# A gate/up pass of a fused transformer kernel from 12-bit parts, with the parts made one pass earlier by ScalarE and accumulating DMAs

## The chip, the cores and the metric

The kernel runs on one core of one Trainium2 chip. A core has five engines with queues of their own: TensorE (PE; its weight loads are shown as PEld), VectorE (DVE), ScalarE (ACT), GpSimd (POOL) and SyncE (SP, which here only issues DMAs). The metric is the time of one execution in microseconds on the device; lower is better. Before the change three runs took 990.1, 990.8 and 993.25 us, median 990.8.

## The reference

Four rows `x[b]` of 512 tokens by 256 channels pass through four residual blocks: a windowed attention with a small convolution (A), a feed-forward block (FFN), a 16-head causal attention (B), and the same FFN with the same weights again.

```python
def _L0_ffn_ref(x, gate_W_packed, gate_scales, up_W_packed, up_scales, down_W_packed, down_scales):
    Wg = dequant_nvfp4(gate_W_packed, gate_scales)
    Wu = dequant_nvfp4(up_W_packed, up_scales)
    Wd = dequant_nvfp4(down_W_packed, down_scales)
    gate = jnp.einsum('th,nh->tn', xt, Wg)
    up = jnp.einsum('th,nh->tn', xt, Wu)
    gelu = jnp.tanh(0.7978845608028654 * (gate + 0.044715 * gate ** 3)) * gate * 0.5 + gate * 0.5
    inter = gelu * up
    out = jnp.einsum('tn,hn->th', inter, Wd)

x = x + _L0_attn_a_ref(_layernorm(x, axis=-1), ...)
x = x + _L0_ffn_ref(_layernorm(x, axis=-1), ...)
x = x + _L0_attn_b_ref(_layernorm(x, axis=-1), ...)
x = x + _L0_ffn_ref(_layernorm(x, axis=-1), ...)
```

The weights are 256 x 2048 (gate, up) and 2048 x 256 (down), everything in float32.

## The kernel before

**Passes.** One FFN pass treats one row b. Its 2048 hidden values are 16 blocks n of 128. For each n there is a gate tile and an up tile of 128 x 512, each summed over two halves `par` of the 256 channels; then gelu on ScalarE (`gs`), a product on VectorE (`it`), and after every eight blocks the down product in four groups of 64/4 matmuls (`po`), added to `X[b]` by VectorE (L977). There are eight passes: f0 to f3 after attention A, and s0 to s3 after attention B.

**Two ways to multiply.** The function `ffn` (from L901) multiplies float32 weights from SBUF directly: the raw weights `Wf["g"]` and `Wf["u"]`, 16 tiles of 128 x 512, named by matrix, `par` and quarter q of the hidden values. f0, f1 and f2 run so. In the other way every factor is split into parts of about 12 bits, in a type that TensorE takes in one go: `high = w * NEAR` rounded, the rest `w - high`, and a correction `w - high * (1 + STEP)`. A tile is then four matmuls (`begin`: forms 0 and 1, two `par` each), a scaling of the PSUM bank by ScalarE (1 + STEP), and two matmuls with form 2 on top (`end`). The activations are split in the same manner into `xs`. f3 and all of s0 to s3 run so, inside `conduct` (`ffn_pass`, L1243 on), with weights read back from DRAM as chunks of 768 KB, one for each n.

**Where the parts come from.** `keep_parts` (L989) takes the 16 raw tiles; ScalarE writes `high` (L997), VectorE the two others (L998, L999), and SyncE stores each as 256 KB into the DRAM tensor `kept` (L1001). Its steps stand beside f2 and window 3. Their room is one slot of the tag "T".

**Order.** `weave` takes work of attention A ("window" b+1) and of the pass f_b together: every step of the window yields a time, and TensorE gets main work for as long. Beside f1 stands window 2, beside f2 window 3. Only TensorE's order is written out there (`manual_schedule(engines=PE_ONLY)`); the framework orders the other engines' queues when the program is built. The window's VectorE half is `window_middle`; its yields are 46.2 us in sum, scaled by (0.79, 1.24, 1.22) for windows 1, 2 and 3. Then come `project` (L714, L720), `turn` (L739, L741), `move` (TensorE, zp, L761), `add` (VectorE, L772) and `norm_rows`, in which GpSimd computes an inverse root (`inv_root`, L102 and L103) and TensorE transposes the normalized rows (L886) that ScalarE copies to `xT` (L892). The next window's `window_front` has a root of its own on GpSimd (L352).

**PSUM.** Until the end of f2 the pool `fbank` has three banks, afterwards four.

```python
        with tc.manual_schedule(engines={mybir.EngineType.PE, mybir.EngineType.DVE}):
            first_slot()
        for b in range(1, 3):
            weave(ffn(f1, i1, b, got[b], f"f{b}", False, False), beside_window(b + 1), 1.0)
```

Of the kernel before, what the change touches and what calls it, by code (L numbers as in the profile page):

```python
# [18 lines left out]
P = 128  # L19
# [20 lines left out]
def hybrid_kernel(  # L40
# [50 lines left out]
    def hold(pool, names):  # L91
        for name in names:
            Wf[name] = [[pool.tile([P, 512], F32, name=f"{name}{par}_{q}") for q in range(4)] for par in range(2)]

    hold(wpool, "d")
    store = ctx.enter_context(tc.tile_pool(name="store", bufs=1, space=bass.MemoryType.DRAM))
# [889 lines left out]
                    )  # L986


    def keep_parts(make):  # L989

        for q in range(4):
            for k, mat in enumerate(("g", "u")):
                for par in range(2):
                    w = Wf[mat][par][q]
                    t = make(f"{mat}{par}_{q}")
                    top = t[:, 0].bitcast(F32)
                    nc.scalar.activation(t[:, 0], w, AF.Copy, scale=NEAR)  # L997
                    nc.vector.tensor_tensor(t[:, 1], w, top, ALU.subtract)  # L998
                    nc.vector.scalar_tensor_tensor(t[:, 2], top, -1.0 - STEP, w, ALU.mult, ALU.add)  # L999
                    for form in range(3):  # L1000
                        nc.sync.dma_start(  # L1001
                            out=kept[q][:, :, k, form, par, :].rearrange("n p c -> p n c"),
                            in_=t[:, form].bitcast(F32).rearrange("p (n c) -> p n c", c=P),
                        )
                    yield 0.0

    class Slot:

# [762 lines left out]
    def scaled(work, by):  # L1771
        for w in work:
            yield w * by
# [31 lines left out]

    got, mine, state = [], [], {}
    with ExitStack() as left:
        hold(left.enter_context(tc.tile_pool(name="wraw", bufs=1, side="left")), "gu")
        aw = left.enter_context(tc.tile_pool(name="aw", bufs=1, side="left"))
        a1 = left.enter_context(tc.tile_pool(name="a1", bufs=1, side="left"))  # L1810
        a2 = left.enter_context(tc.tile_pool(name="a2", bufs=2, side="left"))
# [211 lines left out]
        def beside_window(b):  # L2023

            middle = window_middle(a1, a2, wconst, b, state)
            other = iter(())
            if b + 1 < B:
                xa = window_load(a2, b + 1)
                other = window_front(a1, a2, wconst, b + 1, xa, state)

            if b == 3:
                room = a2.tile([P, 2, 4, 512], F32R, tag="T", name="room")
                made = []

                def make(name):
                    made.append(name)
                    return room[:, len(made) % 2, 0:3]

                other = keep_parts(make)
            yield from between(  # L2040
                scaled(middle, (0.79, 1.24, 1.22)[b - 1]), until(other, state, b + 1) if b + 1 < B else other
            )
            project, turn, move, add = window_back(a1, a2, wconst, b, state)
            for hf in range(2):
                yield from project(hf)
            wait = sum(turn())
            if b + 1 < B:
                next(other)
                wait = 3.5
            yield wait  # L2050
            move()
# [12 lines left out]
        for b in range(1, 3):  # L2064
            weave(ffn(f1, i1, b, got[b], f"f{b}", False, False), beside_window(b + 1), 1.0)

    early.close()
    fbank = ctx.enter_context(tc.tile_pool(name="ps4", bufs=4, space=bass.MemoryType.PSUM))
# [96 lines left out]
```

## Time and profile before

| What | us |
|---|---|
| Median of three runs | 990.8 |
| The profiled execution, its own time | 993.88 |
| its span in the profile | 992.0 |
| f1's first gate matmul | 189.9 |
| f2's first gate matmul | 290.9 |
| f2's last down matmul ends about | 383.2 |
| Parts: first activation, last store issued | 262.3, 342.7 |
| First chunk load of f3 issued | 376.8 |

Mean granted TensorE clock of the execution: 0.991. Line numbers are those of the kernel before. A line of a timeline gives start, length, engine, line, operation, output and inputs, and in brackets the idle time of the engine just before and what ended it. Matmuls are pipelined, so the starts of successive groups tell the pace, not their lengths. Tile names end in the stage: `_f` for f0 to f3, `_s` for s0 to s3. A 128 x 512 float32 matmul counts as two instructions, so a full tile shows as x4; a tile from parts shows as x4 (`begin`) and x2 (`end`).

### The profile page before, as it was taken

How to read it: one execution, taken by the hardware profiler on the slowest of the kernel's cores; microseconds unless marked ns; L12 is line 12 of the kernel's file. 1: busy time of each engine (PE TensorE's matmuls, PEld its weight loads, DVE VectorE, ACT ScalarE, POOL GpSimd, SP SyncE). 2: the span in 40 equal slices, each digit the busy share in tenths (PEclk: the TensorE clock that was granted, in tenths of full speed). 3: DMA queues.
4: the chain of work that ended last, by engine and by line, in shares of the span. 5: the costliest groups of instructions: out<-in, count | busy, mean ns of one | idle time of the engine just before them, and what ended most of it. 6: DMA issues, size and time to landing. Idle time of an engine off the chain costs nothing.

```text
span 992.0 us, 15580 instructions
## 1 busy us (share of the span) xinstructions
PE 960.7 (97%) x5872; PEld 654.0 (66%) x5872; DVE 713.6 (72%) x1626; ACT 454.4 (46%) x806; POOL 137.0 (14%) x263
## 2 busy tenths in 40 slices
PE   8999998999999999899999999999999999999998
PEld 6874647655674666666556666676666677657887
DVE  7889998889899767875876776667775667546211
ACT  3453243040333111665462853746727548475531
POOL 2100000010000013201422123111141111120000
PEclk9899999999999999999999999999999999999999
DMA  5202110000245605331330340522503406134730
GB/s 147 93 25 62 41 45 1 23 1 0 67 124 146 175 12 185 128 128 50 103 104 1 107 149 1 191 76 75 191 1 128 139 11 212 44 128 143 251 124 34
DMA packets 51774, 90.92 MB, mean 92 GB/s; under 512 B 4915, under 2 KB 37963, under 8 KB 51667
## 3 DMA queue, kind: packets, MB, share of 16 engines
q1 hardware_dynamic: 49696, 89.34, 27.8%
q8 instruction: 46, 0.75, 0.3%
q10 hardware_dynamic: 1906, 0.54, 0.2%
q14 instruction: 30, 0.24, 0.1%
q0 software_dynamic: 96, 0.05, 0.1%
HBM read 75.24 MB, written 14.68 MB: 91 GB/s over the span
## 4 chain that ended last, share of the span: by engine, by line
PE 80%; DVE 11%; ACT 4%; DMA 2%; issue 1%; SPq 0%; POOL 0%; DVEq 0%; ACTq 0%
PE po_s L1325 11%; PE pg_f L913 7%; PE pu_f L934 6%; PE pg_s L1269 6%; PE pu_s L1269 6%; PE s L1540 5%; PE po_f L962 4%; PE sT L1574 4%; PE o L1618 4%; PE pu_s L1282 3%; PE qk_b L1453 3%; PE po_f L1325 3%; PE pg_s L1282 3%; PE va L496 2%; PE pg_f L1269 2%; PE v_b L1485 1%
## 5 line engine op out<-in xcount | busy, mean ns | idle before, releaser
L1554 DVE CUSTOM_DVE_ANT_0 junk<-s,mask 128x512 f32<-128x512 f32 (+3 forms) x256 | 125.6, 491 | 54.3 <-PE s L1540 20.7
L1325 PE MATMUL po_s<-d,it_s 128*128 128x256 f32 x512 | 117.8, 383 | 0.6 <-DVE it_s L1312 0.5
L1325 PEld LDWEIGHTS po_s<-d,it_s 128*128 128x128 f32 x512 | 95.3, 190 | 20.4 <-issue 5.2
L1586 ACT ACTIVATE e<-sT 128x1024 f32<-128x1024 f32 (+1 forms) x66 | 64.7, 1006 | 88.7 <-PE sT L1574 88.6
L1593 POOL TENSOR_SCALAR_AFFINE_SELECT e<-e 128x256 f32<-128x256 f32 x128 | 53.4, 429 | 336.9 <-ACT e L1586 311.2
L913 PE MATMUL pg_f<-xT_f,g 128*128 128x512 f32 x192 | 93.1, 607 | 1.0 <-ACT xT_f L889 0.7
L934 PE MATMUL pu_f<-xT_f,u 128*128 128x512 f32 x192 | 91.1, 593 | 0.0
L962 PE MATMUL po_f<-d,it_f 128*128 128x256 f32 x384 | 88.6, 387 | 0.5 <-DVE d L830 0.4
L962 PEld LDWEIGHTS po_f<-d,it_f 128*128 128x128 f32 x384 | 72.9, 193 | 13.3 <-issue 1.8
L925 ACT ACTIVATE gs_f<-pg_f 128x512 f32<-128x512 f32 x48 | 28.6, 595 | 109.9 <-PE pg_f L913 102.3
L1269 PE MATMUL pg_s<-xs_s,chunk_s 128*128 128x512 f32 x256 | 70.8, 398 | 0.5 <-ACT qT L1517 0.5
L1269 PE MATMUL pu_s<-xs_s,chunk_s 128*128 128x512 f32 x256 | 70.7, 398 | 0.5 <-DVE gu_s L1310 0.5
L913 PEld LDWEIGHTS pg_f<-xT_f,g 128*128 128x128 f32 x192 | 35.9, 193 | 44.9 <-issue 35.2
L934 PEld LDWEIGHTS pu_f<-xT_f,u 128*128 128x128 f32 x192 | 36.0, 191 | 42.3 <-issue 40.2
L1269 PEld LDWEIGHTS pu_s<-xs_s,chunk_s 128*128 128x128 f32 x256 | 47.1, 188 | 18.0 <-DVE it_s L1312 1.7
L1269 PEld LDWEIGHTS pg_s<-xs_s,chunk_s 128*128 128x128 f32 x256 | 46.9, 188 | 14.8 <-ACT qT L1517 1.3
L1274 ACT ACTIVATE pu_s<-pu_s 128x512 f32<-128x512 f32 x64 | 37.3, 583 | 41.2 <-PE pu_s L1269 40.4
L1540 PE MATMUL s<-kT,qT 16*128 16x256 f32 (+3 forms) x512 | 50.9, 467 | 3.2 <-ACT qT L1517 1.9
L1296 DVE SCALAR_TENSOR_TENSOR g_s<-g_s,gs_s 128x512 f32<-128x512 f32 x48 | 33.6, 701 | 20.5 <-ACT g_s L1294 20.5
L1274 ACT ACTIVATE pg_s<-pg_s 128x512 f32<-128x512 f32 x64 | 37.3, 583 | 21.5 <-PE pg_s L1269 20.9
L1618 PE MATMUL o<-e,V 128*32 128x256 f32 (+3 forms) x512 | 44.4, 442 | 0.0
L1282 PE MATMUL pu_s<-xs_s,chunk_s 128*128 128x512 f32 x128 | 41.9, 408 | 1.1 <-ACT pu_s L1274 1.1
(281 smaller groups left out, 1739.6 us busy)
## 6 DMA issues: line engine op xcount, KB each, us to landing
chunk_s<-kept SPq DMA_DIRECT2D x64, 768.0 KB
kept<-room SPq DMA_DIRECT2D x48, 256.0 KB
chunk_f<-kept SPq DMA_DIRECT2D x16, 768.0 KB
X<-in_x_dram SPq DMA_DIRECT2D x4, 512.0 KB
out_dram<-X SPq DMA_DIRECT2D x15, 128.0 KB
xa<-in_x_dram SPq DMA_DIRECT2D x28, 64.0 KB
pkg<-in_gate_p_dram SPq DMA_DIRECT2D x4, 256.0 KB
sbg<-in_gate_s_dram SPq DMA_DIRECT2D x4, 256.0 KB
```

What stands on the lines that cost most here:

```text
L913: nc.tensor.matmul(pg, Wf["g"][par][q][:, o : o + P], xT[:, par, :], start=par == 0, stop=par == 1)
L934: nc.tensor.matmul(pu, Wf["u"][par][q][:, o : o + P], xT[:, par, :], start=par == 0, stop=par == 1)
L962: nc.tensor.matmul(po[:, 0:W], inter[k][:, i * P : (i + 1) * P], Wf["d"][par][j // 2][:, (j % 2) * W : (j % 2 + 1) * W], start=k == 0, sto ...
L1269: nc.tensor.matmul(ps(), ch()[:, int(mat == "u"), form, par], xs()[:, form, par], start=k == 0, stop=k == 3)
L1274: step("ACT", 0.585, lambda: nc.scalar.activation(ps(), ps(), AF.Copy, scale=1.0 + STEP), r=[ps], w=[ps], lane="ffn", rank="scale")
L1282: nc.tensor.matmul(ps(), ch()[:, int(mat == "u"), 2, par], xs()[:, 2, par], start=False, stop=par == 1, skip_group_check=True,)
L1325: nc.tensor.matmul(po()[:, 0:W], inter[n]()[:, i * P : (i + 1) * P], Wf["d"][par][j // 2][:, (j % 2) * W : (j % 2 + 1) * W], start=k == 0, ...
L1540: nc.tensor.matmul(pss[hl // 2]()[:, hl % 2, p0 : p0 + n], qT[h0 : h0 + HD, g, i * P : (i + 1) * P], kT[h0 : h0 + HD, g, 0:n], start=True, ...
L1554: step("DVE", 0.155 + n / 960.0 + 0.085, lambda hl=hl, i=i, p0=p0, n=n, h=h, junk=junk: nc.vector.tensor_tensor_reduce(out=junk()[:, 0:n], ...
L1586: step("ACT", 0.16 + 2 * total / 1200.0, lambda: nc.scalar.activation(e()[:, :, 0:total], pss[k]()[:, :, at0:512], AF.Exp), r=[(pss[k], "t ...
L1593: nc.gpsimd.affine_select(out=diag, in_=diag, pattern=[[0, 2], [1, P]], compare_op=ALU.is_ge, fill=0.0, base=0, channel_multiplier=-1,)
L1618: nc.tensor.matmul(o()[h0 : h0 + 32, kt * P : 512], c["V"][:, kt, 4 * g + hl, :], e()[:, hl % 2, p0 : p0 + n], start=kt == 0, stop=kt == 2,)
```

## The change

f2 is run from parts too, by a new generator `ffn_in_parts`. The parts are made beside f1 and window 2 instead of beside f2 and window 3. `keep_parts` no longer uses VectorE: ScalarE makes `less = -high`, `high` and `low = -STEP * high`, SyncE stores them, and GpSimd's queue then adds the raw weight to form 1 in DRAM and form 1 to form 2 in DRAM, by two accumulating DMAs per raw tile. The 16 raw tiles lie in a pool whose tags are reused: the first six hold the room of `xs`, three groups of three that of the three chunk buffers of f2, and one stands alone. Window 3's middle is scaled by 1.05 instead of 1.22.

```diff
+    def hold_in_turn(pool):
+
+        turns = [(name, par, q) for q in range(4) for name in "gu" for par in range(2)]
+        first = pool.tile([P, 6, 512], F32, tag="xs", name="raw_first")
+        rest = [pool.tile([P, 3, 512], F32, tag="chunk", bufs=3, name=f"raw{k}") for k in range(3)]
+        last = pool.tile([P, 512], F32, name="raw_last")
+        spots = [first[:, k] for k in range(6)] + [t[:, k] for t in rest for k in range(3)] + [last]
...
-    def keep_parts(make):
+    def keep_parts(pool):
 
         for q in range(4):
             for k, mat in enumerate(("g", "u")):
                 for par in range(2):
                     w = Wf[mat][par][q]
-                    t = make(f"{mat}{par}_{q}")
-                    top = t[:, 0].bitcast(F32)
-                    nc.scalar.activation(t[:, 0], w, AF.Copy, scale=NEAR)
-                    nc.vector.tensor_tensor(t[:, 1], w, top, ALU.subtract)
-                    nc.vector.scalar_tensor_tensor(t[:, 2], top, -1.0 - STEP, w, ALU.mult, ALU.add)
-                    for form in range(3):
-                        nc.sync.dma_start(
-                            out=kept[q][:, :, k, form, par, :].rearrange("n p c -> p n c"),
-                            in_=t[:, form].bitcast(F32).rearrange("p (n c) -> p n c", c=P),
-                        )
+                    to = [kept[q][:, :, k, form, par, :].rearrange("n p c -> p n c") for form in range(3)]
+                    of = lambda t: t.rearrange("p (n c) -> p n c", c=P)
+                    high = pool.tile([P, 512], F32R, tag="g2", name=f"high_{mat}{par}_{q}")
+                    less = pool.tile([P, 512], F32R, tag="gu", name=f"less_{mat}{par}_{q}")
+                    low = pool.tile([P, 512], F32, tag="gu", name=f"low_{mat}{par}_{q}")
+                    nc.scalar.activation(less, w, AF.Copy, scale=-NEAR)
+                    nc.sync.dma_start(out=to[1], in_=of(less.bitcast(F32)))
+                    nc.scalar.activation(high, w, AF.Copy, scale=NEAR)
+                    nc.sync.dma_start(out=to[0], in_=of(high.bitcast(F32)))
+                    nc.scalar.activation(low, high.bitcast(F32), AF.Copy, scale=-STEP)
+                    nc.sync.dma_start(out=to[2], in_=of(low))
+                    nc.gpsimd.dma_start(out=to[1], in_=of(w), accum_op=ALU.add)
+                    nc.gpsimd.dma_start(out=to[2], in_=to[1], accum_op=ALU.add)
                     yield 0.0
+
+    def in_parts(pool, xT, name):
+
+        xs = pool.tile([P, 3, 2, 512], F32R, tag="xs", name=f"xs_{name}")
+        part = xs.bitcast(F32)
+        for par in range(2):
+            nc.scalar.activation(xs[:, 0, par], xT[:, par], AF.Copy, scale=NEAR)
+            nc.vector.tensor_tensor(xs[:, 2, par], xT[:, par], part[:, 0, par], ALU.subtract)
+            nc.scalar.activation(xs[:, 1, par], part[:, 2, par], AF.Copy, scale=4096.0)
+            nc.vector.tensor_tensor(xs[:, 2, par], part[:, 0, par], part[:, 1, par], ALU.subtract)
+        return xs
+
+    def ffn_in_parts(pool, ipool, ring, b, xT, name, tanh, last):
+
+        xs = in_parts(ring, xT, name)
+        chunks = {}
+
+        def begin(mat, n):
+            if n not in chunks:
+                chunks[n] = ring.tile([P, 2, 3, 2, P], F32R, tag="chunk", bufs=3, name=f"chunk_{name}_{n}")
+                nc.sync.dma_start(out=chunks[n].bitcast(F32), in_=kept[n // 4][n % 4])
+            ps = fbank.tile([P, 512], F32, tag="ps", name=f"p{mat}_{name}_{n}")
+            for k, (form, par) in enumerate(((0, 0), (0, 1), (1, 0), (1, 1))):
+                nc.tensor.matmul(
+                    ps, chunks[n][:, int(mat == "u"), form, par], xs[:, form, par], start=k == 0, stop=k == 3
+                )
+            nc.scalar.activation(ps, ps, AF.Copy, scale=1.0 + STEP)
+            return ps
+
+        def end(mat, n, ps):
+            for par in range(2):
+                nc.tensor.matmul(
+                    ps, chunks[n][:, int(mat == "u"), 2, par], xs[:, 2, par],
+                    start=False, stop=par == 1, skip_group_check=True,
+                )
...
+                    if begun:
+                        close()
+                        yield 0.45
+                    begun = mat, n, ps
...
-        hold(left.enter_context(tc.tile_pool(name="wraw", bufs=1, side="left")), "gu")
+        wraw = left.enter_context(tc.tile_pool(name="wraw", bufs=1, side="left"))
+        hold_in_turn(wraw)
...
-            yield from between(
-                scaled(middle, (0.79, 1.24, 1.22)[b - 1]), until(other, state, b + 1) if b + 1 < B else other
-            )
+            beside = between(scaled(middle, (0.79, 1.24, 1.05)[b - 1]), until(other, state, b + 1) if b + 1 < B else other)
+            yield from between(beside, keep_parts(f1) if b == 2 else iter(()))
...
-        for b in range(1, 3):
-            weave(ffn(f1, i1, b, got[b], f"f{b}", False, False), beside_window(b + 1), 1.0)
+        weave(ffn(f1, i1, 1, got[1], "f1", False, False), beside_window(2), 1.0)
+        weave(ffn_in_parts(f1, i1, wraw, 2, got[2], "f2", False, False), beside_window(3), 1.0)
```

The lines left out of `ffn_in_parts` are the gelu (ScalarE), the product `it` (VectorE) after each `end`, as in `ffn`, and the call of `down` after eight blocks. Each `begin` yields 0.91 us, each `end` 0.45.

More of the change, by code (lines that the diff above doesn't have):

```diff
@@ L93, in hold @@
             Wf[name] = [[pool.tile([P, 512], F32, name=f"{name}{par}_{q}") for q in range(4)] for par in range(2)]
+    def hold_in_turn(pool):
[4 more added lines that the diff above has]
+        spots = [first[:, k] for k in range(6)] + [t[:, k] for t in rest for k in range(3)] + [last]
+        for name in "gu":
+            Wf[name] = [[None] * 4 for _ in range(2)]
+        for (name, par, q), spot in zip(turns, spots):
+            Wf[name][par][q] = spot
     hold(wpool, "d")
@@ new lines, in ffn_in_parts, with close @@
+    def ffn_in_parts(pool, ipool, ring, b, xT, name, tanh, last):
[18 more added lines that the diff above has]
+                )
+        for half in range(2):
+            inter, gates, begun = [], {}, None
+            def close():
+                mat, n, ps = begun
+                end(mat, n, ps)
+                if mat == "g":
+                    gs = pool.tile([P, 512], F32, tag="gs", name=f"gs_{name}_{n}")
+                    g2 = None
+                    if tanh:
+                        nc.scalar.copy(gs, ps)
+                        g2 = pool.tile([P, 512], F32, tag="g2", name=f"g2_{name}_{n}")
+                        nc.scalar.activation(g2, gs, AF.Square, scale=0.044715 ** 0.5)
+                        nc.vector.scalar_tensor_tensor(g2, g2, 1.0, gs, ALU.add, ALU.mult)
+                        nc.scalar.activation(g2, g2, AF.Tanh, scale=0.7978845608028654)
+                    else:
+                        nc.scalar.activation(gs, ps, AF.Gelu_apprx_tanh)
+                    gates[n] = gs, g2
+                else:
+                    gs, g2 = gates.pop(n)
+                    it = ipool.tile([P, 512], F32, tag="it", name=f"it_{name}_{n}")
+                    if tanh:
+                        gu = pool.tile([P, 512], F32, tag="gu", name=f"gu_{name}_{n}")
+                        nc.vector.scalar_tensor_tensor(gu, ps, 0.5, gs, ALU.mult, ALU.mult)
+                        nc.vector.scalar_tensor_tensor(it, g2, 1.0, gu, ALU.add, ALU.mult)
+                    else:
+                        nc.vector.tensor_tensor(it, ps, gs, ALU.mult)
+                    inter.append(it)
+            for n in range(8 * half, 8 * half + 8):
+                for mat in ("g", "u"):
+                    ps = begin(mat, n)
+                    yield 0.91
+                    if begun:
+                        close()
+                        yield 0.45
+                    begun = mat, n, ps
+            close()
+            yield 0.45
+            for _ in down(b, name, half, inter, last):
+                yield 0.86
@@ L2029, in beside_window @@
                 other = window_front(a1, a2, wconst, b + 1, xa, state)
[L2031 to L2039, printed above, removed]
-            yield from between(
-                scaled(middle, (0.79, 1.24, 1.22)[b - 1]), until(other, state, b + 1) if b + 1 < B else other
-            )
+            beside = between(scaled(middle, (0.79, 1.24, 1.05)[b - 1]), until(other, state, b + 1) if b + 1 < B else other)
+            yield from between(beside, keep_parts(f1) if b == 2 else iter(()))
             project, turn, move, add = window_back(a1, a2, wconst, b, state)
```

## The prediction

> **What bounds the kernel now.** I read the page's first two parts, then the chain of waits, then stretches of the span by engine, then TensorE's, VectorE's and GpSimd's own timelines at the places that the change touches.
>
> ```profile
> PE 960.7 (97%) x5872; PEld 654.0 (66%) x5872; DVE 713.6 (72%) x1626; ACT 454.4 (46%) x806; POOL 137.0 (14%) x263
> ...
> PE 80%; DVE 11%; ACT 4%; DMA 2%; issue 1%; SPq 0%; POOL 0%; DVEq 0%; ACTq 0%
> ```
>
> TensorE is busy 97% of the span and holds 80% of the chain that ends last: time is won where TensorE's work shrinks, if nothing else then ends later. In the stretches of the second pass (189 to 290) and the third (291 to 382) the columns are length, then busy time of PE, PEld, DVE, ACT and POOL, granted clock, DMA share, GB/s:
>
> ```profile
> 189.00:262.00 73.00, 73.00 (x307) 41.97 (x307) 63.43 (x107) 22.09 (x39) 3.06 (x1) 1.00 0.00 1
> 262.00:290.00 28.00, 26.87 (x280) 21.05 (x279) 27.23 (x44) 8.55 (x14) 1.20 (x2) 0.94 0.50 142
> 290.00:330.00 40.00, 39.53 (x117) 21.30 (x116) 40.00 (x58) 14.18 (x20) 0.00 (x0) 1.00 0.46 132
> 330.00:370.00 40.00, 40.00 (x245) 23.05 (x244) 24.45 (x44) 8.88 (x15) 0.97 (x1) 1.00 0.30 86
> ```
>
> VectorE is full from 262 to 330, yet TensorE loses only 1.13 us up to 290 and 0.47 in the next 40. GpSimd is nearly empty. So the third pass is paced by matmuls, with VectorE as a close second.
>
> **Fewer passes through the array: -11.5 us.** TensorE's timeline (start, length, instructions), first in the second pass, then in a pass from parts in the tail:
>
> ```profile
> 232.15 1.88 PE L913 MATMUL pg_f<-xT_f,g 128*128 128x512 f32 x4
> 233.87 1.88 PE L934 MATMUL pu_f<-xT_f,u 128*128 128x512 f32 x4
> ```
> ```profile
> 957.29 1.07 PE L1269 MATMUL pg_s<-xs_s,chunk_s 128*128 128x512 f32 x4
> 958.20 0.62 PE L1282 MATMUL pu_s<-xs_s,chunk_s 128*128 128x512 f32 x2
> 958.65 0.61 PE L1269 MATMUL pu_s<-xs_s,chunk_s 128*128 128x512 f32 x2
> ```
>
> A full tile takes 233.87 - 232.15 = 1.72 us, a tile from parts 958.65 - 957.29 = 1.36. The pass has 32 gate and up tiles: 32 x 0.36 = 11.5 us less. The down half (13.81 us per 64 matmuls) is untouched.
>
> **VectorE's share of the parts goes: -2.9 us.** Today 32 VectorE instructions at about 0.69 us (22 us in all) make the parts, nine of them between 267 and 278. They stand in front of the residual addition:
>
> ```profile
> 270.43 0.69 DVE L998 TENSOR_TENSOR room<-u,room 128x512 fp32r<-128x512 f32 x1
> 271.04 1.21 DVE L772 TENSOR_TENSOR X<-X,zp 128x1024 f32<-128x1024 f32 x1
> ```
> ```profile
> 272.31 1.02 PE L426 MATMUL qkv<-bw,yT 32*128 32x96 f32 x26 [1.13 <-DVE X L772]
> ...
> 274.43 9.72 PE L962 MATMUL po_f<-d,it_f 128*128 128x256 f32 x36
> ```
>
> TensorE waits 1.13 us for that addition, and the clock then sags (0.71, 0.50 and 0.94 in the 2 us slices from 274 to 280): 36 down matmuls span 283.99 - 274.43 = 9.56 us, where 36/64 x 13.81 = 7.8 are due. The zp matmuls end at 268.87 and no part would stand in between, so 1.1 + 1.8 us should return; bounds 0 and 2.9, I take 2.9.
>
> **The new beginning of the pass: +1.5.** Four ScalarE and four VectorE instructions split xT ahead of the first matmul. The fourth pass has the same chain: its first split begins at 381.40 and its last needed one ends at 384.57, 3.2 us. Today xT of the third pass is copied by 287.81 and the first pg starts at 290.92: 3.1 us of cover from the second pass's last down matmuls. If VectorE is in a 2.28 us product (L535) at both subtractions, 4.6 us show. Bounds 0 and 5; nearest to the covered case, so 1.5.
>
> **Three banks, now coupled more tightly: +3.** Today a pu bank is asked for again two tiles later, 3.44 us after its last matmul. From parts, one begin (0.91) and one end (0.45) lie between: 1.36 us for VectorE to see it, multiply (0.69) and free it. Products of 1.2 to 2.3 us fill VectorE in the first half of the pass, so a multiply can miss by up to about 0.9 us. Eight tiles at 0.4 give 3. Bounds: 0 (VectorE is some 7 us further ahead than today, ten part instructions fewer by 293) and 7 (eight at 0.9). ScalarE's scaling (0.585) must fit under the next begin, 0.91. Four table loads of 1.28 us lie between 287.8 and 301.9, three of them in the pass, and each now sits in front of a scaling: 0 to 4, I take 1.5.
>
> **The ring has three chunks: +0.5.** A chunk is free one begin and one end after its own pair (4.08 us after its first matmul) and its buffer is due again at 8.16. In the tail the last chunk is issued at 964.28 and DMA activity is over at 968 (share 0.87, then 0.03): about 4.0 us against 4.08. Bounds 0 and 2.
>
> **The end of the pass: +2.** After window 3's last matmuls (zp, ended 368.88) 13.0 us of down work (60 matmuls) cover a fixed chain: addition, norm, and transfers of attention weights that land at 382.3. The middle's factor 1.22 to 1.05 on 46.2 us of yields holds window 3 back less (48.5 us instead of 56.4); with 13.2 us of later yields 61.7 of 71.1 us of pass are spent before zp, 9.4 us stay. 13 - 9.4 = 3.6 us of cover are missing. Bounds 0 and 4 (a new idle may bring its own sag); norm work placed there fills some, so 2.
>
> **The parts beside the second pass: +1, if GpSimd keeps up.** ScalarE gets 48 activations at 0.63 us, 30 us, in a phase where it is busy some 31 of 101: room enough, but each `less` waits until the store before has left its buffer (two stores, issued at 262.93 and 263.44, are through by 266: about 2.5 us), and the xT, aT and gelu copies queue behind it; 0 to 5. SyncE issues 48 stores as before, earlier, behind window 3's xa loads (179.7 to 185.5, needed at 191.4), and 16 chunk loads more behind them. The heavy item is GpSimd's queue: 32 accumulating transfers, the second of each pair waiting for the first to land, ahead of window 3's root (204.4, with 1.7 us until VectorE uses it) and of the third pass's own:
>
> ```profile
> 1.37 0.84 POOL L173 DMA_DIRECT2D wrep<-in_qkv_w_dram  x1 [0.37 <-issue]
> ...
> 2.56 0.61 POOL L175 DMA_DIRECT2D sh<-in_shift_dram  x1
> 3.16 0.63 POOL L198 DMA_DIRECT2D prep<-in_proj_w_dram  x1
> ```
> ```profile
> 276.33 0.20 POOL L102 TENSOR_SCALAR rs_f<-mv_f 128x4 f32<-128x4 f32 x1 [68.83 <-DVE mv_f L849]
> 276.61 1.01 POOL L103 TENSOR_TENSOR rs_f<-rs_f,mhalf 128x4 f32<-128x4 f32 x1
> ```
>
> No accumulating transfer is in this trace. Nearest are GpSimd's three plain ones of 128 rows: 0.61 to 0.84 us to issue, 2.6 to 4.5 us to land. Ours have 512 pieces of 512 B and 256 KB, 0.91 us at the 287 GB/s that the stores reached. Issue: 0.6 (one per transfer) to 2.5 (four times 0.63); taken 1.3. Landing: 2.6 to 6.3 (4.5 and the data twice); taken 4.2. A step of two: 3.2 to 8.8, taken 5.5; sixteen from 189.9 end at 241, 278 or 331. The root at 276.33 has 4.9 us of slack (factors applied by 279.03, transposes in TensorE's order at 283.99), so 281.2 is the deadline, 5.7 us per step: the value taken is in time by 3 us.
>
> On this the Trainium skill's page "SBUF — State Buffer", section "SBUF: two separate sides", speaks against the change: while VectorE runs an instruction that takes both ports, GpSimd can't write descriptors, and an issue of 620 ns became 3100. By it, 32 issues alone would be an estimated 99 us, past the deadline. This trace's nearest row is the root at 204.4, 3.06 us beside a full VectorE against 1.68 at 10.2, and no transfer of GpSimd lies beside dense VectorE work, so I keep the sum by rows.
>
> **Sum.** -11.5 - 2.9 + 1.5 + 3 + 1.5 + 0.5 + 2 + 1 = -4.9. The profiled execution took 993.88 us (span 992.0 and 1.9 around it), 3.1 over the median of 990.8; 993.88 - 4.9 = 989.0 there, 985.9 on the median: **986**. Differences under 0.3% (3 us, 987.8 to 993.8) can't be told from none.
>
> **Rivals.** *GpSimd comes late* (slower): above 5.7 us per step the root, xT and the third pass's first matmul slip by 16 us for each us. For it: the wait between the two transfers, which no other work fills if the queue holds them pairwise, and the DMA engines, which up to the deadline owe 48 x 0.91 = 44 us of stores and 32 times 0.91 to 1.8, 29 to 58 us, of accumulation in 91 us. Against: at 3.2 us per step it would end at 241. At 6.5 us the queue ends at 293.9, 12.7 late: 986 + 12.7 = 999. *The coupling eats it* (slower): the upper ends of beginning, banks, tables, ring and end, 5 + 7 + 4 + 2 + 4 = 22, plus 1, against 14.4: 990.8 + 8.6 = 999; half-way between that and the values taken, 993 to 999, I name 996. For it: VectorE's 40.00 of 40. Against: 22 us of that work are gone. *The gain is hidden* (no change): the transfers of attention weights and the norm after zp set the end anyway, and the sagging clock only moves; 11.5 is met by 3.6 of lost cover, 5 at the beginning and 3 at the banks: 990.8 - 11.5 + 11.6 = 991.
>
> **How the numbers follow.** Forecast 46%, GpSimd late 26%, coupling 16%, hidden 12%. So faster 46%, same 12%, slower 42%. The forecast's own range is 979 (new costs at a third: 9.5 / 3 - 14.4) to 988; to leave out no more than two in ten it goes to 1004, a GpSimd step of 6.8 us.
>
> **What would show it.** Right: chunks in the third pass at 1.36 us per tile; no wait at zp's addition; the rs_f root of the third pass starting within a us of its mv; GpSimd's last transfer issued before it. Wrong: idle TensorE before the xTp transposes or the first pg of the third pass, released by GpSimd; waits on `it` or on scaled banks of more than 7 us in the pass; chunk loads that wait for accumulating transfers. If the issue of one accumulating transfer takes over 2.5 us, the forecast is wrong whatever else holds.

## The result and the profile after

The changed kernel takes 1053.05 us (median; 1051.42 to 1054.16) beside 992.02 (990.1 to 993.44) before: ratio 1.0615, interval 1.0588 to 1.0642. It is 6% slower; the predicted 986 us and its range to 1004 are both missed. The profiled span is 1050.6 us against 992.0.

The page's totals by engine, and the chain that ended last:

```profile
PE 962.6 (92%) x5936; PEld 669.7 (64%) x5936; DVE 699.5 (67%) x1598; ACT 489.7 (47%) x872; POOL 178.1 (17%) x295
...
PE 62%; DVE 7%; ACT 3%; DMA 2%; issue 2%; POOL 0%; SPq 0%; DVEq 0%; ACTq 0%; POOLq 0%
```

TensorE's busy time is what it was (962.6 against 960.7), its share of the span falls from 97 to 92%: the time went into waiting. (f2's matmuls got shorter, but others ran longer: the mean granted clock fell from 0.991 to 0.958, from 150 to 170 us it is 0.59 instead of 1.00.) Four stretches split the span, and every later run is read by them. "Conduct" is the part of the kernel from f3 on; all times are in us, taken from starts rounded to a tenth:

| Kernel | f1's first gate matmul | from there to f2's | f2's to conduct's first | conduct to the end | span |
|---|---|---|---|---|---|
| before | 189.7 | 101.2 | 95.4 | 605.7 | 992.0 |
| after | 235.9 | 112.2 | 92.4 | 610.2 | 1050.6 |

46.2 of the 58.6 us are lost before f1 begins, 11 in f1 and 4.5 in conduct; f2's stretch gains 3.0. TensorE's timeline of the kernel after, around f1's beginning (start, length, instructions, idle time before them and what ended it):

```profile
190.36 4.58 PE L974 MATMUL po_f<-d,it_f 128*128 128x256 f32 x20
231.14 1.08 PE L898 MATMUL xTp_f<-ident,xn_f 128*128 128x128 f32 x4 [36.19 <-DVE xn_f L878]
...
235.86 1.88 PE L925 MATMUL pg_f<-xT_f,raw_first 128*128 128x512 f32 x4
...
272.65 3.78 PE L925 MATMUL pg_f<-xT_f,raw_first 128*128 128x512 f32 x4 [8.56 <-DVE it_f L957]
```

The transposes wait for the normalized rows, and these for GpSimd's root of f1; the 8.56 us in f1 begin with VectorE's wait for window 3's root:

```profile
230.58 1.71 DVE L878 TENSOR_SCALAR xn_f<-X,mv_f,rs_f 128x256 f32<-128x256 f32 x4 [36.06 <-POOL rs_f L867]
...
269.44 0.17 DVE L369 SCALAR_TENSOR_TENSOR mean<-pm,rsa 128x8 f32<-128x8 f32 x1 [11.42 <-POOL rsa L364]
```

GpSimd's timeline shows where the roots were (L1018 and L1019 are the two accumulating transfers of a step, L867 f1's root, L364 window 3's):

```profile
142.55 1.41 POOL L1018 DMA_DIRECT2D kept<-raw_first  x1 [11.34 <-DMA kept<-less_g]
148.39 1.29 POOL L1019 DMA_DIRECT2D kept<-kept  x1 [4.42 <-DMA kept<-raw_first]
149.46 1.53 POOL L1018 DMA_DIRECT2D kept<-raw_first  x1
158.25 1.26 POOL L1019 DMA_DIRECT2D kept<-kept  x1 [7.26 <-DMA kept<-raw_first]
...
228.21 1.26 POOL L1019 DMA_DIRECT2D kept<-kept  x1 [4.73 <-DMA kept<-raw]
228.99 1.55 POOL L867 TENSOR_TENSOR rs_f<-rs_f,mhalf 128x4 f32<-128x4 f32 x1
...
265.86 1.84 POOL L1018 DMA_DIRECT2D kept<-raw_last  x1
266.65 2.76 POOL L364 TENSOR_TENSOR rsa<-off,mhalf 128x8 f32<-128x8 f32 x1
```

The queue begins at 142.55, in the first slot, not at f1, and ends with the issue at 272.58: 131.4 us, 8.2 a step. In most steps GpSimd stands 4 to 8 us until the first transfer has landed. f1's root comes 36 us late. Window 3's root is behind fifteen steps; VectorE waits 11.42 us for it, the product `it` stands behind that in VectorE's queue, and TensorE waits the 8.56 us for `it`. f2's own root is in time.

Some 9 of the other 10 us before f1 are ScalarE's. It writes a part into a room that an earlier store must first have left, and copies that TensorE needs stand behind:

```profile
168.26 0.63 ACT L1012 ACTIVATE less_g<-raw_first 128x512 fp32r<-128x512 f32 x1 [4.80 <-DMA kept<-less_g]
168.79 1.05 ACT L449 COPY T<-qkv 128x512 f32<-128x512 f32 x2
```

Window 1's zp, the last matmuls of the first slot's window, moved from 177.43 to 186.25.

### The profile page after: what moved, and what is told of

Read it like the earlier page. It is cut to its first block, busy times and chain, and to the rows that moved or that the text cites. A ratio compares the mean times of both kernels' runs of the same rounds, so it can differ in the third digit from the quotient of the medians.

```text
span 1050.6 us, 15870 instructions
## 1 busy us (share of the span) xinstructions
PE 962.6 (92%) x5936; PEld 669.7 (64%) x5936; DVE 699.5 (67%) x1598; ACT 489.7 (47%) x872; POOL 178.1 (17%) x295
## 4 chain that ended last, share of the span: by engine, by line
PE 62%; DVE 7%; ACT 3%; DMA 2%; issue 2%; POOL 0%; SPq 0%; DVEq 0%; ACTq 0%; POOLq 0%
PE po_s L1417 11%; PE pg_s L1361 6%; PE pu_s L1361 5%; PE s L1632 4%; PE sT L1666 3%; PE o L1710 3%; PE pu_s L1374 3%; PE po_f L1417 3%; PE qk_b L1545 3%; PE pg_s L1374 3%; PE pg_f L925 2%; PE pg_f L1361 2%; PE v_b L1577 1%; PE po_f L974 1%; PE pu_f L946 1%
## 5 line engine op out<-in xcount | busy, mean ns | idle before, releaser
L1361 PE MATMUL pg_s<-xs_s,chunk_s 128*128 128x512 f32 x256 | 72.1, 404 | 0.5 <-ACT qT L1609 0.5
L1361 PEld LDWEIGHTS pg_s<-xs_s,chunk_s 128*128 128x128 f32 x256 | 48.0, 192 | 15.5 <-issue 1.7
L937 ACT ACTIVATE gs_f<-pg_f 128x512 f32<-128x512 f32 x32 | 19.0, 595 | 75.7 <-PE pg_f L925 72.8
L925 PE MATMUL pg_f<-xT_f,raw_first 128*128 128x512 f32 x64 | 35.3, 676 | 11.1 <-DVE it_f L957 8.6
L1402 DVE SCALAR_TENSOR_TENSOR gu_s<-pu_s,gs_s 128x512 f32<-128x512 f32 x48 | 33.0, 689 | 16.2 <-PE pu_s L1374 15.5
L1374 PE MATMUL pg_s<-xs_s,chunk_s 128*128 128x512 f32 x128 | 42.3, 412 | 0.3 <-ACT pg_s L1366 0.3
L898 PE MATMUL xTp_f<-ident,xn_f 128*128 128x128 f32 x32 | 6.6, 346 | 37.5 <-DVE xn_f L878 37.5
```

The source lines that it names most:

```text
L925: nc.tensor.matmul(pg, Wf["g"][par][q][:, o : o + P], xT[:, par, :], start=par == 0, stop=par == 1)
L1361: nc.tensor.matmul(ps(), ch()[:, int(mat == "u"), form, par], xs()[:, form, par], start=k == 0, stop=k == 3)
L1374: nc.tensor.matmul(ps(), ch()[:, int(mat == "u"), 2, par], xs()[:, 2, par], start=False, stop=par == 1, skip_group_check=True,)
```

## The experiments

Three explanations compete. Theory T: GpSimd's queue stands in front of the roots. Rival R1: ScalarE's copies and SyncE's stores set the time. Rival R2: it is the transfers' load on the DMA engines, and the pass's own couplings. All runs start from the kernel after. The columns are f1's first gate matmul and the three stretches of the profiled execution; ratios are to the kernel before on the same chip, with their intervals.

| Run | f1 | f1 to f2 | f2 to conduct | to the end | median us | ratio |
|---|---|---|---|---|---|---|
| e1_no_adds | 188.2 | 97.8 | 94.1 | 608.7 | 989.4 | 0.9995 (0.9971 to 1.0019) |
| e2_held | 184.1 | 141.7 | 97.9 | 608.6 | 1033.4 | 1.0438 (1.0406 to 1.0469) |
| e3_roots | 208.9 | 101.4 | 93.4 | 608.6 | 1014.2 | 1.0246 (1.0217 to 1.0276) |
| e4_lag | 205.4 | 106.8 | 93.2 | 607.2 | 1021.4 | 1.0336 (1.0300 to 1.0372) |
| e5_held_roots_lag | 182.5 | 133.0 | 92.9 | 606.3 | 1018.8 | 1.0310 (1.0276 to 1.0345) |
| e6_pool_adds | 195.0 | 106.1 | 92.2 | 609.0 | 1004.6 | 1.0157 (1.0138 to 1.0177) |
| e7_pool_adds_held | 183.6 | 119.2 | 93.2 | 607.3 | 1005.0 | 1.0162 (1.0141 to 1.0183) |
| e8_raw_f2 | 191.8 | 98.0 | 93.5 | 605.6 | 990.4 | 1.0003 (0.9987 to 1.0019) |
| e9_roots_one_add | 198.1 | 100.8 | 94.4 | 606.4 | 1004.0 | 1.0141 (1.0102 to 1.0180) |
| e10_spread | 193.2 | 109.4 | 94.3 | 609.0 | 1007.8 | 1.0203 (1.0163 to 1.0242) |
| e11_long_rows | 221.7 | 108.6 | 97.4 | 606.0 | 1036.2 | 1.0476 (1.0455 to 1.0497) |
| e12_long_rows_roots_lag | 208.6 | 107.8 | 97.3 | 610.1 | 1022.3 | 1.0320 (1.0290 to 1.0349) |
| e13_exps_free | 190.0 | 97.8 | 94.2 | 608.7 | 992.1 | 1.0030 (1.0014 to 1.0046) |
| e14_exps_free_early | 190.2 | 97.8 | 92.9 | 605.6 | 989.8 | 1.0009 (0.9990 to 1.0027) |
| e15_vector_adds | 190.9 | 100.7 | 95.1 | 605.6 | 996.1 | 1.0075 (1.0055 to 1.0095) |
| e16_pool_adds_exps_free | 198.0 | 105.1 | 94.3 | 605.4 | 1006.6 | 1.0171 (1.0154 to 1.0188) |

The first column scatters by some 4 us among kernels with the same first slot (188.2 and 191.8 in e1 and e8), so less than that is not read from it. A profiled execution can also lie off its kernel's median: that of the kernel before took 993.88 us (medians 989.0 to 990.5 on the chips of these runs), that of e4 1014.3, 7 us under its median.

**e1: the transfers taken out.**

```diff
-                    nc.gpsimd.dma_start(out=to[1], in_=of(w), accum_op=ALU.add)
-                    nc.gpsimd.dma_start(out=to[2], in_=to[1], accum_op=ALU.add)
```


> Left out: the 32 accumulating transfers of keep_parts, so the second and third parts of the weights stay without their sums; everything else of the change stands. Theory T (GpSimd's queue of accumulating transfers stands in front of f1's root at L867 and window 3's root at L364): the 36.19 us wait before f1's transposes and the 8.56 us in f1's matmuls are gone, f1's first gate matmul comes at 190 to 198 instead of 235.86, and the whole takes 990 to 1003 us. Rival R1 (ScalarE's copies and SyncE's stores, put into the same stretch, set it): the ScalarE waits on stores stay, f1 begins after 215, total over 1030. Rival R2 (the transfers' load on the DMA engines and f2's own coupling set it): f1 begins between, f2's stretch grows; 1005 to 1030.

As T expected, and a little below its ranges: 989.4 us, and f1 no longer waits for a root:

```profile
188.21 1.99 PE L925 MATMUL pg_f<-xT_f,raw_first 128*128 128x512 f32 x4 [0.35 <-ACT xT_f L901]
```

The transfers are the whole loss; ScalarE's 48 activations and the 48 stores alone cost nothing that shows. But nothing is gained either: level with the kernel before.

**e2: the steps held back to f1.** Every instruction of a step waits for f1's root and its second transposed copy.

```diff
+                        for ins in (state["f1", "root"], state["f1", "xT"]):
+                            hold_on.enter_context(tc.issue_after(ins.ins))
```


> Computes all. Each step of keep_parts waits for f1's root and f1's second transposed copy, so no store and no accumulating transfer is issued before about 190. Theory T: f1 begins on time (189 to 193), but sixteen steps at the measured 8.2 us from 190 end at about 321, with window 3's root (wanted near 250) and f2's root (wanted near 277) in the same queue: f2 begins 25 to 45 us late, total 1025 to 1040; were a step to fall to 5.5 us once the first slot's own loads are past, it would be 995 to 1010. Rival R1 (ScalarE and SyncE): stores begin later too, so total 995 to 1005 with the GpSimd still late but no TensorE wait on it. Rival R2: a wait on a chunk or on an operand of f2 stands in TensorE's rows, not one on a root.

As T expected. The steps run from 187.66 to 315.10 (8.0 us each), f2's root follows only then, and f2 begins at 325.81:

```profile
313.84 1.27 POOL L1019 DMA_DIRECT2D kept<-kept  x1 [6.24 <-DMA kept<-raw_last]
315.18 0.20 POOL L114 TENSOR_SCALAR rs_f<-mv_f 128x4 f32<-128x4 f32 x1
```

This is the rival *GpSimd comes late* as the prediction told it, at 8.0 us a step.

**e3: the roots moved away.** f1's, f2's and window 3's roots by Newton steps on VectorE.

```diff
-            nc.gpsimd.tensor_tensor(rs, off, mhalf, ALU.pow)
+                newton_root(rs, off, a1.tile([P, 8], F32, tag="nt", name=f"nt{b}"), 1.0)
```


> Computes all. The roots of f1, of f2 and of window 3 are taken on VectorE by Newton steps instead of GpSimd's power; the transfers stay where they are in GpSimd's queue. Theory T: nothing that TensorE waits for is left behind the transfers, f1 begins at 193 to 203 (the ScalarE waits on stores in the first slot, about 9 us, stay), window 3's mean no longer waits, total 990 to 1005. Rival R1 (ScalarE and SyncE set it): f1 begins after 220, total over 1030. Rival R2 (DMA load): f1 on time but the stretch from f1's first to f2's first gate matmul stays 11 us longer than before, total 1005 to 1020.

Between the theories. 3.7 of the 6.2% are gone and no wait is on a root; 24 us are left, 19 of them before f1. TensorE's waits between 130 and 215 us (what waited, what ended it, sum, times, longest):

```profile
PE pg_f L930 <- ACT xT_f L906: 7.0, 1, 7.0
PE qkv L441 <- ACT T L458: 4.3, 1, 4.3
PE aTp L735 <- ACT aT L731: 4.2, 2, 3.5
PE qkv L441 <- ACT yT L400: 2.4, 1, 2.4
```

All are copies of ScalarE, which stood at rooms of parts. So R1's waits are the second loss, which the late root had partly covered. But e1 has the same copies and stores and loses nothing: up to 182 us its ScalarE waits for a room at most 1.68 us at a time, in e3 up to 5.55. The long waits come with the accumulating transfers.

**e4: the wait between the two transfers filled.**

```diff
+                    issue(to[1], of(w))
+                    second.append((to[2], to[1]))
+                    if len(second) > 2:
+                        issue(*second.pop(0))
```


> Computes all. The second accumulating transfer of a step is issued two steps after its first, in a fixed order, so that GpSimd need not stand until the first one has landed. Theory T with the step set by the landing: the step falls from 8.2 us to 3 to 5 us, f1's root runs at 195 to 210 instead of 228.99, total 1005 to 1030. If the step is set by the DMA engines' load instead (rival R2), it stays at 7 to 8.5 us and the total at 1045 to 1060. Rival R1 (ScalarE and SyncE) expects the step to fall and the total to stay over 1040.

The total is in T's range, the step is not: it falls to 6.1 us (139.74 to 236.9), not to 3 to 5. f1's root runs at 193.30, and the same ScalarE waits follow (6.6, 4.7, 3.3 us). So GpSimd's standing is only a part of the step; what holds the rest at 6 us is asked in e9 to e12.

**e5: all three together**, the steps held back by f1's second transposed copy alone.

```diff
+                        for ins in (state["f1", "xT"],):
+                            hold_on.enter_context(tc.issue_after(ins.ins))
```


> Computes all. Three edits together: each step of keep_parts waits for f1's second transposed copy, the roots of f1, f2 and window 3 are VectorE's, and the second transfer of a step is issued two steps after its first. If GpSimd's queue and its steps of 8.2 us were the whole loss: f1 begins at 184 to 188 (in the two runs with the first slot free of the transfers it began at 184.07 and 188.21), sixteen steps at the 6.1 us of the lagged run end at about 285, f2 begins at 282 to 290 and the total is 984 to 995 us. If the transfers also cost by their DMA load or by keeping raw rooms from f2's chunks, a wait on a chunk or on a ScalarE copy of 5 to 15 us stands at f2's begin, total 995 to 1008.

Worse than both expectations: f1 at 182.54, its stretch 133.0 us. With DMA busy shares of 1.11 and 1.19 from 182 to 271 (a share adds up the packets' times, which overlap here), ScalarE stands at stores, gelu comes late (TensorE waits 23.9 us for `gs`, VectorE 30.1). What is kept out of the first slot is paid in f1.

**e6 and e7: GpSimd adds by itself, in place and held back.** Two additions and three plain stores a step.

```diff
+                    nc.gpsimd.tensor_tensor(less, w, high.bitcast(F32), ALU.subtract)
+                    nc.gpsimd.tensor_tensor(low, less, low, ALU.add)
```


> Computes all. GpSimd makes the two small parts itself from the raw weight and ScalarE's high part (two additions over 128x512 in place of two accumulating transfers), three plain stores follow; the place of the steps is the change's. If the price lay in the transfers' landing time, which holds GpSimd, and not in having GpSimd or the stores there at all: an addition takes 1 to 3 us by the 0.51 us of an addition over 128x128, a step 2 to 6 us, f1's root at most some us late, f1 begins at 188 to 198, total 985 to 1000. If the stores and ScalarE set it, f1 begins after 200 as in the runs with VectorE's roots (208.86) and with the lag (205.44), total 1005 to 1015. A slower VectorE beside the additions would show in its mean times of the first slot and of f1.

> Computes all. As the run with GpSimd's own additions, and the steps wait for f1's root and f1's second transposed copy. If the first slot's loss (the first zp at 175 to 188 us in the runs with stores in that slot, at 171.81 in the held one) is the stores' and ScalarE's, f1 begins at 183 to 186; sixteen steps of 2 to 6 us end by 200 to 280, window 3's root waits for at most a step; f2 begins at 281 to 288, total 981 to 992. If what is lost before f1 comes back as a wait in f1 or f2, the total stays at 989 to 1000.

Both totals miss: 1004.6 and 1005.0. A step takes 5.4 us, roots are a few us late at most, but f1's stretch grows to 106.1 and 119.2. VectorE's groups in f1 (count, busy, mean ns), before and in e7:

```profile
L639 DVE TENSOR_TENSOR tv<-tv 128x1024 f32<-128x1024 f32 x4 | 4.9, 1214 | 0.0
```
```profile
L651 DVE TENSOR_TENSOR tv<-tv 128x1024 f32<-128x1024 f32 x4 | 9.1, 2284 | 0.0
```

This addition takes 1.9 times as long beside GpSimd's (others of the same size 1.07 to 1.25 times); VectorE is busy 107.6 us in f1's stretch against 85.6 in e1, about the 21 us by which the stretch is longer.

**e8: the pass itself undone.** No transfers, and f2 from the raw weights again.

```diff
-        weave(ffn_in_parts(f1, i1, wraw, 2, got[2], "f2", False, False), beside_window(3), 1.0)
+        weave(ffn(f1, i1, 2, got[2], "f2", False, False), beside_window(3), 1.0)
```


> Left out: the accumulating transfers, as in the first run (989.4 us); and undone: the second pass runs from the raw weights again as before the change (factor 1.22 too), so only the early making of the parts is left. What the second pass in parts is worth by itself is the difference to that first run. By the prediction's matmul term the pass in parts saves 11.5 us less 3 to 8 of its own waits, so this run is 993 to 998 us. If the waits that the pass in parts brings (7.2 us of TensorE idle between its first matmul and conduct) and the work that covers the window's end eat the whole, it is 985 to 991, level with the first run.

990.4 us, level with e1: the pass in parts is worth nothing here. Its stretch is 93.5 us from raw weights and 94.1 from parts. The kernel before, from raw weights too, has 95.4 there; it also makes the parts beside it on VectorE.

**e9: half of the transfers.** e3, and of each step only the first transfer.

```diff
-                    nc.gpsimd.dma_start(out=to[2], in_=to[1], accum_op=ALU.add)
```


> Left out: the second accumulating transfer of each step, so the third part stays without its sum. The roots of f1, f2 and window 3 are VectorE's, as in the run at 1014.2 us, where ScalarE's waits for the room of its parts (stores not yet landed) still made f1 20 us late. If the stores are late because the accumulating transfers fill the DMA engines, halving them takes 8 to 17 us of that away: f1 begins at 191 to 200, total 993 to 1005. If ScalarE's rooms turn too slowly whatever the load, f1 still begins at 205 to 210, total 1008 to 1016.

f1 at 198.13, 1004.0 us, both in the range for the load: some 40% of e3's loss (2.5% to 1.5% over e1) goes with half of the transfers. ScalarE's work is the same in both, so its waits hang on the DMA engines' load. The queues of e3 between 130 and 290 us (packets, MB, share of 16 engines; q0 holds GpSimd's transfers):

```profile
q0 software_dynamic: 16896, 8.39, 47.0%
q1 hardware_dynamic: 27064, 15.21, 33.1%
```

Per MB the accumulating transfers take 2.6 times the DMA engine time of the rest (47.0 / 8.39 = 5.6% against 33.1 / 15.21 = 2.2%).

**e10: the steps spread out**, six over the first slot and ten over f1, with e3's and e4's edits.

```diff
+                behind = [-90, -75, -66, -55, -42, -18, 0, 1, 2, 4, 5, 7, 8, 10, 11, 13, 13]
...
+                        hold_on.enter_context(tc.issue_after(slot[n] if n < 0 else gelus[min(n, len(gelus) - 1)]))
```

A negative number counts back over the first slot's VectorE instructions, another is a block of f1.


> Computes all. VectorE's roots, the second transfer two steps after its first, and the sixteen steps spread: six behind instructions of VectorE from about 126 to 182 us, ten behind gelus of f1 from about 188 to 262. If the loss that is left with VectorE's roots (24 us) is ScalarE waiting for stores because the steps are bunched where the DMA engines are full, the spread takes most of it: f1 begins at 186 to 194, f1's stretch is 98 to 106 us, total 988 to 1002. If the load of the transfers costs wherever they lie, what is gained before f1 comes back in f1's stretch, total 1008 to 1018.

1007.8, just under the second range: better than e3's 1014.2, whose steps are bunched (and which lacks e4's edit), but f1's stretch is 109.4 us. The load costs wherever it lies.

**e11 and e12: longer rows in memory.** A part as rows of 2 KB; e12 with e3's and e4's edits.

```diff
-    kept = [store.tile([4, P, 2, 3, 2, P], F32, name=f"kept{q}") for q in range(4)]
+    kept = [store.tile([P, 2, 3, 2, 4, P], F32, name=f"kept{q}") for q in range(4)]
```


> Computes all. Only the layout of the kept parts in memory differs: a form of a weight lies in rows of 2 KB for each partition instead of four pieces of 512 B, so stores and accumulating transfers move long rows, and a chunk's load gathers twelve pieces of 512 B for each partition instead of one of 6 KB. If the transfers are dear by their many short pieces: the landing falls from 7.5 and 5.6 us to 3 to 5, a step from 8.2 to 4 to 6 us, f1's root runs at 190 to 210 instead of 228.99 and f1 begins at 195 to 215 instead of 235.86. If they are dear by their bytes (read, add, write back), the step stays at 7 to 8.5 us and f1's begin at 225 to 240. The chunks' loads get slower in the second pass and in conduct, which I bound at 0 to 30 us on the total; so the places of f1's and f2's first matmuls tell, not the total: 1010 to 1060.

> Computes all. The long rows, VectorE's roots, and the second transfer two steps after its first. If short pieces are what fills the DMA engines: ScalarE's waits for stores are gone, f1 begins at 188 to 196 as without the additions (188.21 and 191.81), its stretch takes 98 to 104 us, and what is left over the run without the additions is the chunks' loads: f2's stretch 94 us plus 0 to 10. If the bytes fill them, f1 begins at 200 to 210 as with VectorE's roots alone (208.86), total over 1008.

In e11 an issue falls from 1.82 and 1.26 us to 1.21 and 0.84, the step from 8.2 to 7.2 (140.98 to 256.3), f1's root to 215.55, f1's begin to 221.70: between the two expectations, nearer to the bytes. The transfers' share of DMA engine time from 130 to 290 us falls from 48.0 to 38.6%. In e12 f1 begins at 208.56, as with e3's short rows, though e4's edit is in it too. So most of the price is in the bytes, and by that share about a fifth in the pieces. f2's stretch is 3 to 5 us longer, with 3.2 and 4.3 us of waits for chunks, which now come in short pieces.

**e13 and e14: why the pass gains nothing.** In e1's trace VectorE stands 15.5 us in f2's first half; ScalarE's timeline there shows why (`ek` are window 3's exps):

```profile
313.00 0.59 ACT L1071 ACTIVATE gs_f<-pg_f 128x512 f32<-128x512 f32 x1
313.61 1.28 ACT L603 ACT_TABLE_LOAD   x1
314.90 1.15 ACT L603 ACTIVATE ek<-sc 128x512 f32<-128x512 f32 x2
```

Their operands were ready at 284.6 and 295.2. `window_middle` puts the exps behind the last ScalarE instruction emitted: before the change a copy of `keep_parts`, now the eighth gelu of the pass. A new theory: this hides the gain. Both runs leave the transfers out, as e1 does.

```diff
-            queue_behind(w["power"](br), behind)
+            ins = w["power"](br)
+            if b < 3:
+                queue_behind(ins, behind)
...
-            beside = between(scaled(middle, (0.79, 1.24, 1.05)[b - 1]), until(other, state, b + 1) if b + 1 < B else other)
+            beside = between(scaled(middle, (0.79, 1.24, 0.85)[b - 1]), until(other, state, b + 1) if b + 1 < B else other)
```

The factor is e14's alone.


> Left out: the accumulating transfers, as in the first run (989.4 us). Window 3's exps are no longer put behind the last ScalarE instruction emitted. If their lateness (314.9 us, operands ready at 284.6 and 295.2) is what hides the gain: they run at 284 to 300, VectorE's idle time of 15.5 us in the pass's first half is gone, z is ready 5 to 15 us earlier and the total is 979 to 986 us. If TensorE's own waits (chunks, the parts of x, gelu: 7.2 us) and the place of window 3's matmuls in its order set the stretch, the exps come early and the total stays at 986 to 991.

> Left out: the accumulating transfers. Window 3's exps free as in the run beside it, and the factor of the window's middle 0.85 instead of 1.05, so that its projection and zp stand some four blocks earlier in TensorE's order. If the window's chain is free with the exps early, zp comes 5 to 9 us earlier, more of the last projection is left to cover the window's end, total 976 to 984 us. If the stretch is TensorE's own work and waits, the total is within 3 us of the run beside it; if VectorE's chain is not ready then, TensorE waits at the projection's transposes and it is slower than the run beside it by 2 to 8 us.

The theory falls. In e13 the exps run at 286.38 and 299.71, window 3's attention is done at 325.0 instead of 342.2, and the total is 992.1. In e14, factor 0.85, zp also starts 65.1 us after f2's first matmul instead of 75.2, yet the stretch is 92.9 us. So neither the exps nor the window's end sets it; what is left is TensorE's own work and waits, which no run takes apart further. Sums of the stretch in e8 and in e14 (length; busy time of PE, PEld, DVE, ACT, POOL):

```profile
sum 93.50, PE 93.21 PEld 57.28 DVE 61.02 ACT 19.88 POOL 6.47; mean PE 23.30 PEld 14.32 DVE 15.26 ACT 4.97 POOL 1.62
```
```profile
sum 92.90, PE 85.46 PEld 68.05 DVE 63.66 ACT 39.29 POOL 6.53; mean PE 17.09 PEld 13.61 DVE 12.73 ACT 7.86 POOL 1.31
```

TensorE's busy time falls by 7.7 us and its idle time rises from 0.3 to 7.4. The named waits of e14 there:

```profile
PE pg_f L1044 <- DVE it_f L1083: 2.1, 2, 1.6
PE pg_f L1044 <- ACT xs_f L1029: 2.0, 1, 2.0
PE pg_f L1044 <- ACT gs_f L1073: 0.8, 1, 0.8
PE pu_f L1044 <- ACT gs_f L1073: 0.8, 1, 0.8
```

**e15 and e16: complete kernels with the parts made in other ways.** e15: both small parts by VectorE; e16: by GpSimd as in e6; both with free exps.

```diff
+                    nc.vector.tensor_tensor(less, w, high.bitcast(F32), ALU.subtract)
+                    nc.vector.tensor_tensor(low, less, low, ALU.add)
```


> Computes all. The two small parts are made by VectorE (two operations of 0.69 us over 128x512 a step, 22 us in all) with three plain stores, at the change's place beside the first slot and f1; window 3's exps free. VectorE is busy for 85.6 of the 97.8 us of f1's stretch without additions, so 22 us more make it 105 to 112 us long: total 990 to 1002 us. If much of it fits into VectorE's idle time of the first slot (8.8 us and less) it is 984 to 990; GpSimd and the DMA engines are no longer in it.

> Computes all. GpSimd's own additions as in the run at 1004.6 us, and window 3's exps free. If the order of the exps costs what the two runs without additions will show (0 to 10 us), the total is that much lower: 994 to 1004 us. It does not come below the kernel before, as GpSimd's additions make VectorE's two-operand operations slower (1.21 to 2.28 us for one over 128x1024) and the stores still hold ScalarE.

e15, 996.1 us, is the fastest complete kernel after the change; f1's stretch, expected at 105 to 112, is 100.7 us, as half of VectorE's work found idle time in the first slot. It stays 0.75% behind the kernel before. e16, 1006.6, is above its range and gains nothing over e6. Nothing here points to a version that beats the kernel before: e1 and e8 carry no additions at all and are level with it.

## Why the prediction was wrong

**The step that failed is the one priced at +1, "the parts beside the second pass, if GpSimd keeps up".** It cost about 61 us (1.0615 against e1's 0.9995). Three things in it were wrong.

*Where the queue begins.* I let it begin at 189.9, since the steps stand beside f1 in the program. Only TensorE's order is written out there; the framework moved the steps into the first slot, to 142.55. Hence the wrong deadline: f2's root was in time, while f1's root, which I had not thought of, and window 3's, which I had named without a price, came behind up to fifteen steps. e2 puts the queue where I had it, and there it fails as well.

*The price of a step.* Issue was taken at 1.3 and measured at 1.26 and 1.82; landing, counted from the start of the issue, was taken at 4.2 and measured at 7.6 for the first transfer (L1018), on which the queue waits in each step (5.6 for L1019). That makes a step of 8.2, inside its bounds of 3.2 to 8.8 but far from the 5.5 taken. Landing had been scaled from small transfers on empty DMA engines; here shares of 0.91 to 0.97 stand from 140 to 230.

*What the load does to others.* "ScalarE: 0 to 5" held for the copies themselves (e1) but not beside loaded DMA engines, where the rooms of its parts come free late: 19 us before f1 in e3. Rooms, and not only queues, tie ScalarE to the DMA engines. Of the 6.2% that e1 wins back, the roots alone give 3.7 (e3); the other 2.5 are what e9 ties to this load.

The rival *GpSimd comes late* named the mechanism with its threshold of 5.7 us a step; its price of 13 us was too low because its 6.5 us a step was. The page "SBUF — State Buffer" of the Trainium skill, section "SBUF: two separate sides", gives the 3100 ns for one DMA from GpSimd overlapped with a VectorE `tensor_copy`. As the price of every issue beside VectorE it does not fit this case: L1018 and L1019 take 1.3 to 1.8 us while VectorE is busy 19.39 of 20 us (140 to 160) and 1.26 and 1.83 while it does nothing (200 to 230). The cost was the landing.

**The other steps.** The matmul pitch was right only where nothing waits: a tile from parts then takes 1.37 us in f2.

```profile
348.04 0.82 PE L1044 MATMUL pg_f<-xs_f,chunk_f 128*128 128x512 f32 x2
...
352.68 1.08 PE L1044 MATMUL pg_f<-xs_f,chunk_f 128*128 128x512 f32 x4
...
354.05 1.07 PE L1044 MATMUL pu_f<-xs_f,chunk_f 128*128 128x512 f32 x4
...
374.65 13.98 PE L974 MATMUL po_f<-d,it_f 128*128 128x256 f32 x64
```

The first sixteen tiles together take 374.65 - 348.04 = 26.6 us, 1.66 each (27.7 in e1), where sixteen raw tiles at 1.72 take 27.5: half of the pass gains a microsecond, not 5.8.

In the sum, -11.5 met 8.5 us of priced costs, a net of -3.0 for f2's stretch, and 95.4 to 92.4 is what was measured. That agreement is partly luck. By e8, 1.9 us of it go with VectorE's work on the parts, which left this stretch too and which the sum had not counted here; the pass itself changes it by -1.1 (kernel after) to +0.6 us (e1). Of the waits that were priced, the beginning has 0.9 us, the banks (gelu, product and scaling together) 3.2 and the ring 0.6 (1.9 in e1). The end of the pass was right in the place and wrong in the price: 44 down matmuls follow zp where 60 did, as foreseen, but TensorE waits only 0.5 us there, and from zp's end to conduct it is 14.5 us instead of 17.4. Against it, zp comes no earlier (74.2 us after f2's first matmul, 74.3 before), though only the sixteen down matmuls more ahead of it (3.5 us) stand against the 11.5: some 8 us are lost up to there.

-2.9 for VectorE's parts is borne out in its stretch: without the additions f1's takes 97.8 us instead of 101.2, and the wait at zp's addition is gone. In the total it does not show: e8, which has this and not the pass in parts, is level with the kernel before (0.9987 to 1.0019). Two small slips stand in the prediction: f1's first gate matmul is at 189.69, not 189.9, and the lower end of its range is 979.6 by its own sum.

So, without the failed step, the change would have come to 989.4 (e1), inside the range but no change that can be told. That is the number of the rival *hidden* (991, at 12%) rather than the forecast's 986, but not its mechanism: of its terms only the 3 us at the banks were paid, not the 5 at the beginning nor the 3.6 of lost cover, and an earlier zp (e14) changed little. The gain goes in TensorE's small waits and slower tiles before zp.

**Not settled.** Conduct to the end takes 605.4 to 610.2 us in kernels that are the same there. In part it is the clock: after one wait of 1.68 us, sixteen `v_b` matmuls take 3.72 us in the kernel before, e8, e14 and e15, and 5.16 to 5.41 in the kernel after, e1 and e13, with a granted clock of 0.50 in their first 2 us in the kernel after (464.56 to 466.56) and 1.00 in the kernel before. Why it sags in some and not in others was not tried. e1 loses 3.1 us to e8 in this part, so that the two are level holds only to within that. Open, too, is why TensorE's busy time in f2 falls by 7.7 us (e14 against e8) and not by 11.5.

## What to carry to other kernels

Before work is put on an engine that seems empty (GpSimd 14% here), look for the small instructions in its queue that others wait for, and ask where the framework will put the new ones: if the order is not written out, they can land in front of any of these. Price a transfer by its landing under the load that the change itself makes, and follow which engine's rooms it holds; a queue in which each second transfer waits for its first pays the landing every time. A pass that gets shorter on the bound engine gains only what its new waits leave: 11.5 us of matmuls became 7.7 us less work and 7.1 us more idle time.

## What the runs showed of the hardware

- Accumulating transfers of 256 KB into DRAM take 2.6 times the DMA engine time per MB of the other transfers beside them (e3); rows of 2 KB instead of 512 B take a third off an issue (1.82 to 1.21 us), a fifth off their DMA engine time (48.0 to 38.6%) and 12% off the step (e11).
- GpSimd's two-operand additions over 128x512 take 1.27 to 2.1 us in the mean beside VectorE and make some of VectorE's about twice as slow, 2.28 instead of 1.21 us over 128x1024 (e7). GpSimd's DMA issues do not: VectorE is busy 88.2 us in e5's f1 against 85.6 in e1, and e5 has the roots on VectorE too.
